# A graph-network kernel: column copies from octet 5 to the last octet, the second copy of x loaded an octet sooner, and the end in another order

## The chip, the cores and the metric

The kernel runs on one core of one Trainium2 chip. The metric is device time in microseconds (us), lower is better. A core has TensorE (PE, with its weight loads as PEld), VectorE (DVE), ScalarE (ACT), GpSimd (POOL) and SyncE (SP); POOL, SP and ACT also issue DMAs. Each engine works through its own instructions in order.

## What is computed

One layer of a graph network with a residual and a layer norm, over 12,500 nodes of 64 features and 400,000 edges with 16 features each; the edges come sorted by destination.

```python
def _L0_gnn_ref(x, edge_index, edge_attr, W1, b1, W2, b2, W3, b3):
    src, dst = (edge_index[0], edge_index[1])
    m_in = jnp.concatenate([x[src], x[dst], edge_attr], axis=-1)
    h = jax.nn.silu(m_in @ W1 + b1)
    messages = jax.nn.silu(h @ W2 + b2)
    agg = jax.ops.segment_sum(messages, dst, num_segments=x.shape[0])
    node_in = jnp.concatenate([x, agg], axis=-1)
    return jax.nn.silu(node_in @ W3 + b3)
...
x = _layernorm(x + _L0_gnn_ref(x, edge_index, edge_attr_16, ...), axis=-1)
```

## The kernel before

**Octets.** The edges are cut into 3,125 tiles of 128, and eight tiles make an octet: 391 octets (`NO`), numbered 0 to 390, the last with five tiles. One turn of the main loop `for o in range(NO + 2)` in `windows` stands for one octet. Two tiles make a pair, so an octet has four pairs, the last octet three. Many steps of one turn belong to neighbouring octets: gathers are issued three octets ahead (`AHEAD`), the second layer comes two later, the sums four, adding them into `agg` six. For the last eight octets (`DRAIN`) these lags are 1, 2 and 3, so some turns there do two second layers.

**Where the source rows come from.** `x[src] @ W1` for a tile can come in one of three ways. (1) A gather (`gather`, line 448): POOL issues one indirect DMA per tile that fetches 128 rows; up to octet 11 (`RAW` = 12) from `x` itself, from then on from `pa`, a table of products that the start writes to DRAM (`table`). (2) Column copies (`columns`, lines 367 and 369): the core holds two copies of `x` turned round, `xs` and `x2`, and ACT or DVE copies single columns of them, two edges at a time, into a tile `cx` that stands for a whole pair of tiles (256 edges, 128 copies). Before each 8 (ACT) or 16 (DVE) copies the engine loads the addresses into registers. (3) Single rows that SP copies (`rows`). A pair served by (2) or (3) needs two gathers fewer.

**What sets how many.** `shares` says how many edges' worth of columns an engine copies in an octet: ACT 80 in four octets of five and else 64, DVE 96 in seven of ten and else 64, none before octet `BEGIN`. From the running sums, `pairs` gives each engine a list of octets: when 256 more edges are done by octet `o`, a pair of octet `o + 2` is theirs, up to `len(octs) - QUIET - 2`. So `BEGIN` and `QUIET` set the first and the last octet with copies. The copies of an octet stand in fixed places between its other work: on ACT one block ahead of the first layer's silu (`h`, line 557) and one ahead of the second's (`m`, line 572); on DVE a block ahead of `xw` and `oh`, and two behind.

**An octet on its way.** `compare_nodes` (`eh`) and `turn`/`turned` (`ph`, `oh`) make one-hot matrices of the destinations. `first_layer` turns the gathered rows into PSUM (L550), multiplies the copied columns (L553) and adds the one-hots' product (L554); ACT makes `h`. `second_layer` (L566, L568) and ACT make `m`; `add_up` (L581, `pg`) sums over destinations; `add_window` (L592) adds that into `agg`.

**Nodes.** Groups of 512 nodes are finished behind the edges: `node_begin`, `node_x`, `node_sums` on PE, `node_silu` on ACT, `node_add`, `node_stats`, then `root` (a square root on ACT with its own function table), `inverse`, `divide` and `store`. The last two groups are `rest` (512 nodes) and `rest + 1` (212 nodes). In the kernel before, `node_sums(rest)` to `node_stats(rest)` and `limits` (bounds on the indices, which tell whether the general path has to run) stand in turn 390 ahead of its first layer; `verdict` and all of `rest + 1` come last, and root, inverse, divide and store of both groups together.

**Order.** PE, ACT, DVE and SP run in the order in which the loop is written (`manual_schedule`); POOL's gathers follow their own list. A gather waits for a free buffer `ga` (five of them) and for the landing of the gather eight before it.

**Start.** ACT issues the loads of `xs` (turns 0 and 1) and `x2` (`resident2`, turns 2 to 4) in pieces of 2,048 columns, 0.5 MB each; DVE clears the other halves of both tiles in turns 1 to 5 (line 812); turns 1 to 7 make the table `pa`.

## Time and profile before

| | |
|---|---|
| time of three runs | 3284.28 us median (3284.22 to 3288.53) |
| profiled execution | 3281.77 us, span from first to last instruction 3280.0 us |
| mean granted TensorE clock | 0.712 |
| busy: ACT, POOL, PE, DVE | 3106.6, 2462.5, 2460.8, 2063.0 us |
| gathers on POOL | 94 from `x`, 2501 from `pa` |
| column copies | ACT 14464, DVE 16256 |
| HBM read | 135.31 MB |

How to read it: a busy share is a mean over the whole span. Issue of DMAs, register loads and waits are not counted as busy, so an engine can be taken up without being busy. The rows of a timeline give start, duration, engine, line, operation and, in brackets, how long the engine had been idle before and what ended that.

### The profile page before, as it was taken

Reading aid. Unit: us, or ns where it says so; the run is one execution under the profiler, and the core shown is the slowest. Engines: PE = TensorE matmul, PEld = TensorE weight load, DVE = VectorE, ACT = ScalarE, POOL = GpSimd, SP = SyncE. Lnnn points to the kernel's source line nnn. Section 1 sums busy time; section 2 is a strip of 40 time slices with the busy share of each in tenths; the row PEclk is TensorE's granted clock in tenths of the full one; section 3 lists DMA queues with packets and bytes.
Section 4 is the critical chain, followed back from the end, with each engine's and each line's share of the span. In section 5 each row is a group of like instructions: output and inputs, shape, how many; then the busy total and the mean of one; then the engine's idle time right before and its main releaser. Section 6 shows DMA issues by size and latency. Waiting matters only on the chain. (4 is left out here: it accounts for less than half of the span.)

```text
span 3280.0 us, 88619 instructions
## 1 busy us (share of the span) xinstructions
PE 2460.8 (75%) x15346; PEld 1722.2 (53%) x15346; DVE 2063.0 (63%) x18554; ACT 3106.6 (95%) x15306; POOL 2462.5 (75%) x2603
## 2 busy tenths in 40 slices
PE   7776777777778778777777776777778877877786
PEld 5554555545555555555555554545555555555454
DVE  5566666666666666666666666666666666666662
ACT  2899999999999999999999999999999999999992
POOL 7777777777777777777777777777777777777775
PEclk7777667777666776676776777767677676667767
DMA  6211111111111111111111111111111111111111
GB/s 148 53 39 40 46 39 40 46 39 40 45 45 44 42 43 41 41 43 39 48 43 42 42 42 41 42 42 46 45 40 43 40 42 43 40 47 46 39 41 37
DMA packets 160767, 147.72 MB, mean 45 GB/s; under 512 B 103706, under 2 KB 113678, under 8 KB 159422
## 3 DMA queue, kind: packets, MB, share of 16 engines
q0 software_dynamic: 83040, 85.20, 11.7%
q1 hardware_dynamic: 62648, 47.00, 5.3%
q10 hardware_dynamic: 14502, 9.75, 1.4%
q14 instruction: 450, 3.69, 0.3%
q8 instruction: 127, 2.08, 0.3%
HBM read 135.31 MB, written 6.40 MB: 43 GB/s over the span
## 5 line engine op out<-in xcount | busy, mean ns | idle before, releaser
L448 POOL DMA_INDIRECT ga<-pa,sc x2501 | 2372.4, 949 | 762.7 <-issue 649.9
L367 ACT ACTIVATE cx<-xs,x 128x1 f32 x14464 | 2786.9, 325 | 24.0 <-issue 17.7
L369 DVE TENSOR_TENSOR cx<-xs,x 128x4 uint8 x16256 | 1309.3, 154 | 1095.2 <-issue 1075.1
L581 PEld LDWEIGHTS pg<-eh,m 128*64 128x64 f32 x6250 | 281.9, 175 | 928.0 <-DVE agg L592 758.6
L581 PE MATMUL pg<-eh,m 128*64 128x48 f32 x6250 | 336.4, 262 | 467.1 <-DVE agg L592 465.1
L568 PE MATMUL p<-w2d,h 128*128 128x128 f32 x3126 | 641.1, 369 | 0.0
L568 PEld LDWEIGHTS p<-w2d,h 128*128 128x128 f32 x3126 | 543.5, 262 | 159.0 <-issue 159.0
L554 PE MATMUL p<-oh,xw 128*128 128x512 f32 (+1 forms) x758 | 575.2, 853 | 0.0
L550 PE MATMUL p<-ident,ga 128*128 128x128 f32 x1251 | 313.6, 370 | 118.6 <-DMA ga<-pa,sc 117.9
L515 PE MATMUL ph<-identb,eh 128*96 128x128 bf16 x1563 | 221.6, 285 | 158.0 <-DVE oh L525 154.2
L550 PEld LDWEIGHTS p<-ident,ga 128*128 128x128 f32 x1251 | 229.3, 197 | 144.0 <-issue 126.0
L557 ACT ACTIVATE h<-p 128x512 f32<-128x512 f32 x391 | 242.0, 619 | 51.9 <-PE p L554 32.7
L572 ACT ACTIVATE m<-p 128x512 f32<-128x512 f32 x391 | 242.3, 620 | 43.6 <-PE p L568 38.3
L515 PEld LDWEIGHTS <-eh 128*96 128x96 bf16 x1563 | 160.4, 166 | 211.5 <-DVE oh L525 198.4
L525 DVE COPY oh<-ph 96x512 f32<-96x512 f32 x391 | 263.1, 673 | 1.6 <-PE ph L515 1.6
L472 PE MATMUL mm<-w1bb,xr 65*96 65x128 f32 x782 | 230.0, 390 | 6.2 <-DMA xr<-in_xt 3.8
L497 DVE TENSOR_TENSOR eh<-wrow,dc 128x384 f32<-128x384 f32 x392 | 212.4, 542 | 9.3 <-PE pg L581 5.5
L566 PE MATMUL p<-b2r,one 3*128 3x512 bf16 x391 | 188.4, 482 | 31.3 <-ACT m L572 31.1
L554 PEld LDWEIGHTS p<-oh,xw 128*128 128x128 f32 x758 | 173.9, 282 | 0.0
L472 PEld LDWEIGHTS mm<-w1bb,xr 65*96 65x96 f32 x782 | 145.8, 239 | 7.7 <-DMA xr<-in_xt 4.0
L553 PE MATMUL p<-cx,w1d 128*128 128x128 f32 x478 | 122.9, 365 | 0.0
L477 DVE TENSOR_TENSOR xw<-mm,mask 96x128 f32<-96x128 f32 x391 | 108.0, 276 | 17.4 <-PE mm L472 17.4
(106 smaller groups left out, 971.5 us busy)
## 6 DMA issues: line engine op xcount, KB each, us to landing
rx<-pa SPq DMA_DIRECT2D x6400, 0.2 KB
ga<-pa,sc POOLq DMA_INDIRECT x2501
oh<-in_attr SPq DMA_DIRECT2D x130, 192.0 KB
xr<-in_xt SPq DMA_DIRECT2D x391, 24.0 KB
cxi<-in_src_pair SPq DMA_DIRECT2D x240, 1.0 KB
xs<-in_xt ACTq DMA_DIRECT2D x6, 512.0 KB
pa<-v ACTq DMA_DIRECT2D x12, 256.0 KB
x<-in_xt ACTq DMA_DIRECT2D x6, 512.0 KB
```

The source lines that it names most:

```text
L367: nc.scalar.activation(cols[key][:, k:k + 1], word(i, xb, XADDR), AF.Identity, bias=word(i + 4, x2b, X2ADDR))
L369: nc.vector.tensor_tensor(t[:, 4 * k:4 * k + 4], at(i, xb, XADDR), at(i + 4, x2b, X2ADDR), op=OP.max)
L448: nc.gpsimd.indirect_dma_start(out=ga[:, i, :], out_offset=None, in_=x if o < RAW else pa[:, :], in_offset=bass.IndirectOffsetOnAxis(ap=sc ...
L472: nc.tensor.matmul(pw[:E, :], winrow[o], w1bb.rearrange("k s m -> k (s m)"), start=True, stop=True)
L515: nc.tensor.matmul(ph[:E, i, :], eh[:, i, :, 1], identb, start=(i == 0), stop=(i == k - 1), skip_group_check=True)
L525: nc.vector.tensor_copy(oh[:E, :], ph[:E, :(n + 1) // 2].rearrange("p i e -> p (i e)"))
L550: nc.tensor.matmul(p1[:, i, :], g2.rearrange("p s d -> p (s d)"), ident, is_transpose=True, start=(i == c), stop=False, skip_group_check=True)
L554: nc.tensor.matmul(p1[:, :k], xw[o % 3], oh, start=False, stop=True, skip_group_check=True)
L557: nc.scalar.activation(h[:, :k], p1[:, :k], AF.Silu)
L568: nc.tensor.matmul(p2[:, 2 * i:2 * i + 2, :].rearrange("p s d -> p (s d)"), h[:, i, :], w2d, start=False, stop=(i == k - 1), skip_group_ch ...
L572: nc.scalar.activation(m[:, :n2], p2[:, :n2], AF.Silu)
L581: nc.tensor.matmul(pg[s * D:(s + 1) * D, :], m[:, i, :], eh[:, i // 2, :, s], start=(i < 2), stop=(i >= n - 2), skip_group_check=True)
```

## The change

Five things. `BEGIN` goes from 6 to 5 and `QUIET` from 3 to 0, so the copies start one octet sooner and go on to serve the last octet. The loads of `x2` come in turns 1 to 3 instead of 2 to 4, and the clearing of the halves in turns 1 to 4, four pieces a turn, instead of 1 to 5. The end of group `rest` (sums, silu, add, statistics) and `limits` move from turn 390 to turn 389, ahead of its first layer; its root is now worked out on DVE by `newton` (twelve small operations) instead of on ACT, and its divide follows at once. `verdict` and the store of `rest` come in turn 390 behind the first layer, so only group `rest + 1` is left for the end. And of a store, the rows beyond the last multiple of 16 (5 of the last group's 53) go by ACT's queue instead of SP's.

```diff
--- before.py
+++ after.py
@@ -30,7 +30,7 @@
 THIRD = 4
 LAST = 6
 RAW = 12
-BEGIN = 6
+BEGIN = 5
 TABLES = 7
 ACOLS = (48, 32)
 VCOLS = (32, 0, 32, 32)
@@ -43,7 +43,7 @@
 HALF = 6144
 OVER = 304
 TURN = 195
-QUIET = 3
+QUIET = 0
 DRAIN = 8
 LAG = CT * P // 32
 AHEADS = 256
@@ -650,6 +650,20 @@
         def root(q0, q1):
             nc.scalar.activation(rstd[:, q0 * G:q1 * G], mv[:, q0 * G:q1 * G, 1], AF.Sqrt, bias=eps)
 
+        hb = nv.tile([P, G], F32, name="hb")
+        sq = nv.tile([P, G], F32, name="sq")
+
+        def newton(q):
+            y = rstd[:, q * G:(q + 1) * G]
+            nc.vector.tensor_scalar(hb, mv[:, q * G:(q + 1) * G, 1], 1e-5, -0.5, op0=OP.add, op1=OP.mult)
+            bits = y.bitcast(I32)
+            nc.vector.tensor_scalar(bits, hb.bitcast(I32), 1, None, op0=OP.logical_shift_right)
+            nc.vector.tensor_scalar(bits, bits, -1.0, float(0x5f3759df + 0x3fc00000), op0=OP.mult, op1=OP.add)
+            for _ in range(3):
+                nc.vector.tensor_tensor(sq, y, hb, op=OP.mult)
+                nc.vector.tensor_tensor(sq, sq, y, op=OP.mult)
+                nc.vector.scalar_tensor_tensor(y, sq, 1.5, y, op0=OP.add, op1=OP.mult)
+
         def inverse(q0, q1):
             nc.vector.reciprocal(rstd[:, q0 * G:q1 * G], rstd[:, q0 * G:q1 * G])
 
@@ -662,9 +676,9 @@
         def store(q):
             c, n = groups[q]
             to, p = out[c:c + n, :].rearrange("(p i) d -> p i d", i=G), n // G
-            for a, b in ((0, p // 16 * 16), (p // 16 * 16, p)):
+            for a, b, eng in ((0, p // 16 * 16, nc.sync), (p // 16 * 16, p, nc.scalar)):
                 if b > a:
-                    nc.sync.dma_start(to[a:b], v[a:b, q % (2 * RB)])
+                    eng.dma_start(to[a:b], v[a:b, q % (2 * RB)])
 
 
 
@@ -769,8 +783,8 @@
                 if o < 2:
                     for c in parts[2:5] if o == 0 else parts[5:]:
                         resident(c)
-                if 2 <= o < 5:
-                    for c in parts[3 * o - 6:3 * o - 3]:
+                if 1 <= o < 4:
+                    for c in parts[3 * o - 3:3 * o]:
                         resident2(c)
                 if o == 3:
                     for s in range(2):
@@ -805,7 +819,7 @@
                     add_window(q)
                 if o == 1:
                     relative(0, CT, SCT)
-                for k in range(3 * o - 3, 3 * o) if 1 <= o < 6 else []:
+                for k in range(4 * o - 4, 4 * o) if 1 <= o < 5 else []:
                     if k < 2 * len(parts):
                         c = parts[k // 2]
                         t, w = (x2[:D], N) if k % 2 else (xs[D:], NP)
@@ -824,15 +838,22 @@
                     behind()
                     for q in folds[NO]:
                         add_window(q)
+                if o == NO - 2:
                     for i in range(G):
                         node_sums(rest, i)
                     node_silu(rest)
                     node_add(rest)
                     for i in range(G):
                         node_stats(rest, i)
+                    newton(rest)
+                    for i in range(G):
+                        divide(rest, i)
                     bad = limits()
                 if o < NO:
                     first_layer(o)
+                if o == NO - 1:
+                    verdict(bad)
+                    store(rest)
                 for f, a in todo.get(o, []) if o < NO else []:
                     if f is node_silu:
                         f(*a)
@@ -883,16 +904,15 @@
                 for q in folds.get(i, []):
                     add_window(q)
             assert NO not in todo
-            verdict(bad)
             for i in range(G):
                 node_sums(rest + 1, i)
             node_silu(rest + 1)
             node_add(rest + 1)
             for i in range(G):
                 node_stats(rest + 1, i)
-            root(rest, NG)
-            inverse(rest, NG)
-            for q in range(rest, NG):
+            root(rest + 1, NG)
+            inverse(rest + 1, NG)
+            for q in range(rest + 1, NG):
                 for i in range(G):
                     divide(q, i)
                 if q == NG - 1:
```

On POOL, the number of gathers falls by six:

```order
-L448 DMA ga<-in_x,sc 128x64 x94
-L448 DMA ga<-pa,sc 128x64 x2501
```

```order
+L448 DMA ga<-in_x,sc 128x64 x92
+L448 DMA ga<-pa,sc 128x64 x2497
```

ACT has one pair more (128 copies), DVE two (256). With the octets' numbers from `pairs`, a gather's count by octet from 381 to 390 is 8, 4, 8, 8, 4, 8, 8, 6, 8, 5 before and 4, 8, 8, 4, 8, 8, 4, 6, 8, 3 now.

On DVE, turns 386 and 387 (`cx` is the tile of copied columns, `cxi` the addresses, `oh` the next octet's one-hots), the difference of the two orders:

```order
 L592 TENSOR_TENSOR agg<-agg,pg 128x48 x2
 L497 TENSOR_TENSOR eh<-wrow,dc 128x384
-L477 TENSOR_TENSOR xw_169<-mm,mask 96x128
-L525 COPY oh<-ph 96x512
+L350 TENSOR_LOAD cxi
+L369 TENSOR_TENSOR cx<-xs,x_100 128x4 x16
+L477 TENSOR_TENSOR xw_169<-mm,mask 96x128
+L525 COPY oh<-ph 96x512
+L350 TENSOR_LOAD cxi
+L369 TENSOR_TENSOR cx<-xs,x_100 128x4 x16
+L350 TENSOR_LOAD cxi
+L369 TENSOR_TENSOR cx<-xs,x_100 128x4 x16
```

Where these turns had no copies, there are now 16 ahead of the next octet's `xw` and `oh` and 32 behind them; turns 383 and 384 get the same, turn 385 gets 16 and 16, and 16 remain in turn 387.

On DVE, around the last octet's one-hots (`oh` with 384 columns), before:

```order
L525 COPY oh<-ph 96x512
L660 TENSOR_SCALAR v<-v,mv,rstd 128x64 x4
L592 TENSOR_TENSOR agg<-agg,pg 128x48
L525 COPY oh<-ph 96x384
L660 TENSOR_SCALAR v<-v,mv,rstd 128x64 x4
```

and now, the last twelve rows of what stands there:

```order
L674 TENSOR_SCALAR v<-v,mv,rstd 128x64 x4
L721 TENSOR_SCALAR xs<-rowi 128x144 x3
L724 TENSOR_TENSOR xs<-xs,wb 128x391
L726 TENSOR_REDUCE lim<-lims 128x1
L727 TENSOR_REDUCE lim<-lims 128x1
L728 TENSOR_REDUCE lim<-xs 128x1
L729 TENSOR_REDUCE lim<-xs 128x1
L731 TENSOR_SCALAR bad<-lim 128x1
L732 TENSOR_SCALAR bad<-lim 128x1
L733 TENSOR_SCALAR bad<-lim 128x1
L734 TENSOR_SCALAR bad<-lim 128x1
L525 COPY oh<-ph 96x384
```

Between L592 and `oh` there are now group `rest`'s add, four pairs of statistics, `newton`, four divides (the first row here) and `limits`.

On PE, the last two octets (`p` of L550 to L554 is a first layer, of L566 and L568 a second, L630 to `wrow` is `node_sums(rest)`), before:

```order
L566 MATMUL p_197628<-b2r,one_120 128x512
L568 MATMUL p_197628<-w2d,h 128x128 x4
L630 MATMUL wrow<-w3s,agg 128x64 x4
L550 MATMUL p_197670<-ident,ga 128x128 x3
L554 MATMUL p_197670<-oh,xw_169 128x384
```

and now:

```order
L566 MATMUL p_199637<-b2r,one_120 128x512
L568 MATMUL p_199637<-w2d,h 128x128 x4
L550 MATMUL p_199646<-ident,ga 128x128 x2
L553 MATMUL p_199646<-cx,w1d 128x128
L554 MATMUL p_199646<-oh,xw_169 128x384
```

The four products of `node_sums(rest)` have left the way between octet 389's second layer and octet 390's first; they stand ahead of octet 389's first layer. One of octet 390's gathered pairs has become a pair of copied columns.

## The prediction

> **What bounds the kernel now.** I read the page first, then the gathers' line, the waits of POOL and ACT, the stretches around the end, and the timeline from 3180 us on.
>
> ```profile
> PE 2460.8 (75%) x15346; PEld 1722.2 (53%) x15346; DVE 2063.0 (63%) x18554; ACT 3106.6 (95%) x15306; POOL 2462.5 (75%) x2603
> ...
> L448 POOL DMA_INDIRECT ga<-pa,sc x2501: 940/944/1377, 122.0 to 3255.9; - x193
> ...
> POOL ga L448 <- issue: 676.1, 2217, 0.3
> POOL ga L448 <- PE p L545: 2.0, 2, 1.7
> ...
> ACT m L572 <- PE p L568: 6.5, 11, 1.4
> ```
>
> ACT looks like the bound with 95%, but POOL with its 75% is the engine that never rests. Its 2501 gathers start from 122.0 to 3255.9 us, one every (3255.9 - 122.0) / 2500 = 1.2536 us: 0.944 us of work and 0.30 us of "issue" behind each. In the waits hardly one is longer than those 0.3 us; the longest is 1.7 us. So the last gather's time is about the number of gathers times 1.25 us, whatever the other engines do, as long as buffers come free. The last row is ACT's longest wait for PE in total from 600 to 3100 us: 6.5 us in 2500. ACT too is full there, and hardly behind POOL; the two are balanced.
>
> What happens at the end:
>
> ```profile
> 3180.00:3200.00 20.00, 15.34 (x91) 10.65 (x91) 12.00 (x99) 18.97 (x93) 15.12 (x17) 0.65 0.15 33
> 3200.00:3220.00 20.00, 15.78 (x82) 11.06 (x81) 2.96 (x11) 3.17 (x6) 15.12 (x17) 0.52 0.17 40
> 3220.00:3240.00 20.00, 15.49 (x141) 10.30 (x139) 6.06 (x21) 6.37 (x9) 15.12 (x17) 0.80 0.21 56
> ...
> 3239.64 0.94 POOL L448 DMA_INDIRECT ga<-pa,sc  x1 [0.30 <-issue]
> 3248.55 0.37 PE L515 MATMUL ph<-identb,eh 128*96 128x128 bf16 x3
> 3249.66 0.94 POOL L448 DMA_INDIRECT ga<-pa,sc  x1 [0.30 <-issue]
> 3252.20 0.45 PE L550 MATMUL p<-ident,ga 128*128 128x128 f32 x1 [2.19 <-DMA ga<-pa,sc]
> 3254.44 0.60 ACT L557 ACTIVATE h<-p 128x512 f32<-128x512 f32 x1 [6.28 <-PE p L554]
> 3258.45 1.16 PE L568 MATMUL p<-w2d,h 128*128 128x128 f32 x8
> 3259.44 1.98 PE L630 MATMUL wrow<-w3s,agg 128*128 128x64 f32 x8
> 3261.02 0.49 PEld L550 LDWEIGHTS p<-ident,ga 128*128 128x128 f32 x3
> 3262.43 0.49 ACT L557 ACTIVATE h<-p 128x384 f32<-128x384 f32 x1 [0.60 <-PE p L554]
> 3263.67 0.49 DVE L707 TENSOR_SCALAR xs<-rowi 128x144 f32<-128x144 int32 x3
> 3264.22 0.49 ACT L572 ACTIVATE m<-p 128x384 f32<-128x384 f32 x1 [1.30 <-PE p L568]
> 3266.13 0.19 DVE L592 TENSOR_TENSOR agg<-agg,pg 128x48 f32 x1
> 3266.47 0.84 PE L581 MATMUL pg<-eh,m 128*64 128x48 f32 x10 [2.34 <-DVE agg L592]
> 3267.61 1.11 PE L630 MATMUL mm<-w3s,agg 128*53 128x64 f32 x8 [0.17 <-DVE agg L592]
> ```
>
> The columns of the stretches are PE, PEld, DVE, ACT, POOL, the granted clock, the DMA share and GB/s. At 3200 us the copies end: ACT falls from 18.97 to 3.17 us in 20, DVE from 12.00 to 2.96, and POOL stays at 15.12. From there POOL alone sets the time: octet 389's last gather starts at 3249.66, PE waits 2.19 us for it, and `h` follows at 3254.44. Behind that comes a chain of single steps to the end, of which the change shortens three.
>
> **The change part by part.** The sum is made against the profiled execution (span 3280.0, time 3281.77); it is 2.51 us below the median of the runs, 3284.28, and I take the same difference off both.
>
> *Gathers, -5.0 us.* Up to octet 389 there are now four fewer (2586 instead of 2590), so its last one starts 4 x 1.2536 = 5.0 us sooner, at 3244.65. The two that octet 390 saves, 2.5 us more, gain nothing: the last now starts at 3255.9 - 7.5 and lands at 3250.9, and PE gets to it at 3254.6 (below).
>
> *The copies that replace them, 0.* At the start ACT's 40 new copies and DVE's 48 fall into idle time:
>
> ```profile
> 79.86 0.60 ACT L557 ACTIVATE h<-p 128x512 f32<-128x512 f32 x1 [4.63 <-PE p L545]
> 98.21 0.60 ACT L572 ACTIVATE m<-p 128x512 f32<-128x512 f32 x1 [2.98 <-PE p L568]
> 77.96 0.69 DVE L544 COPY m<-mm 128x512 f32<-128x512 f32 x1 [5.29 <-PE mm L542]
> 84.19 0.20 DVE L592 TENSOR_TENSOR agg<-agg,pg 128x48 f32 x1 [4.75 <-PE pg L581]
> 87.95 4.56 ACT L367 ACTIVATE cx<-xs,x 128x1 f32 x24 [0.85 <-issue]
> ...
> 3162.39 1.31 DVE L369 TENSOR_TENSOR cx<-xs,x 128x4 uint8 x16 [0.69 <-issue]
> 3165.12 1.29 DVE L369 TENSOR_TENSOR cx<-xs,x 128x4 uint8 x16 [1.42 <-issue]
> ```
>
> 24 of ACT's copies last 4.56 us and stand where it waited 4.63, 16 last two thirds of that, 3.0, where it waited 2.98. DVE needs 3165.12 - 3162.39 = 2.73 us for 16 with their register load, and waited 5.29 and 4.75. At the end ACT's other 88 copies go to the two octets in which it had come to rest. DVE gets 208 more, 13 blocks or 35 us, in turns 382 to 387. From 3200 to 3240 us it was idle 40 - 2.96 - 6.06 = 31 us. So DVE comes out of these turns about 35 - 31 = 4 us later than now, near 3232 in turn 387. Octet 388's last gather, at 3239.64 - 5.0 = 3234.6, lands 2.5 us later (as 3249.66 to 3252.20 shows for octet 389), at 3237, and is what its first layer waits for. Bounds: nothing, or 4 us when that slack is not there. I take nothing.
>
> A rule of the Trainium skill speaks against more copies: in "SBUF — State Buffer", section "Who interferes with whom", a VectorE instruction with two inputs in SBUF keeps out a GpSimd instruction that reads SBUF. By that rule the new copies would lengthen gathers. The stretches above bear on it: 17 gathers take 15.12 us beside 12.00 us of DVE work as well as beside 2.96. It is a rival below.
>
> *The end in another order, -2.7 us.* On PE, octet 390's first layer no longer stands behind `node_sums(rest)`: it can start when the second layer before it ends, 3258.45 + 1.16 = 3259.61, instead of 3261.02, -1.4 us; a pair of copied columns costs some 0.3 us more than the gathered pair it replaces (an estimate between nothing and 0.5: two products of 128 columns in place of one turned pair). That makes -1.1. What was in the way goes ahead of octet 389's first layer, where PE waits for gathers anyway, so its 1.98 us are covered.
>
> ```profile
> 3256.88 0.60 ACT L572 ACTIVATE m<-p 128x512 f32<-128x512 f32 x1 [1.83 <-PE p L568]
> 3257.53 0.67 PE L581 MATMUL pg<-eh,m 128*64 128x48 f32 x16 [0.75 <-ACT m L572]
> 3261.45 0.38 ACT L636 ACTIVATE z<-wrow 128x256 f32<-128x256 f32 x1 [1.15 <-PE wrow L630]
> 3261.87 0.42 DVE L642 TENSOR_TENSOR v<-xa,z 128x256 f32<-128x256 f32 x1 [3.42 <-ACT z L636]
> 3265.88 0.15 DVE L717 TENSOR_SCALAR bad<-lim 128x1 f32<-128x1 f32 x1
> 3271.61 1.87 DVE L660 TENSOR_SCALAR v<-v,mv,rstd 128x64 f32<-128x64 f32 x8
> L667 SPq DMA_DIRECT2D out<-v x26: 331/375/874, 894.3 to 3274.0; - x26
> ```
>
> On DVE the same group and `limits` now stand ahead of the last `oh`. Their length from the rows of the end: add and statistics 3261.87 to 3263.67, 1.8 us; four divides 1.0; `limits` 3263.67 to 3266.13, 2.5; `newton` has no row: twelve operations of 128 x 4 at 0.06 (four tiny ones take from 3265.88 to 3266.13) to 0.23 us (a divide, 1.87 / 8), 0.7 to 2.8, and I take 2.0, since they depend on each other. Together 7.3 us. The sums can start once octet 390's `ph` is done: at 3248.92 now, and some 4.2 us sooner then, a little less than the gathers, for the copies' sake: 3244.7. With 1.98 for the sums and 0.38 for the silu, DVE starts at 3247.1 and `oh`, after 0.6 of its own, ends near 3255.0. PE wants it 0.5 us after 3259.6 - 5.0, at 3255.1. Hidden, with no slack: late by up to 2 us if `newton` is at its upper bound or the sums start later.
>
> `limits` out of the last stretch: `pg` of octet 390 waits 2.34 us for the add L592, which stood behind `limits` on DVE until 3266.13. From `m` to `pg` are 2.25 us now; one octet before it was 3257.53 - 3256.88 = 0.65. That gives -1.6.
>
> *The last divides and stores, -1.6 us.* Four divides instead of eight: half of 1.87, -0.9. SP's last issue starts at 3274.0 and takes up to 0.87 us; it now stands on ACT beside SP's: -0.7 (between -0.4 and -0.9). The root of `rest + 1` with its table load stays; `verdict` and the store of `rest`, in turn 390 now, have nothing behind them on PE and SP but this same end, and are covered by its layers.
>
> *The loads of x2 an octet sooner, +0.8 us.*
>
> ```profile
> 40.00:60.00 20.00, 18.43 (x107) 13.79 (x106) 14.26 (x15) 4.48 (x8) 14.02 (x16) 0.84 1.00 214
> 23.74 1.76 DVE L812 MEMSET x<- 64x2048 f32 x1 [0.46 <-issue]
> 51.65 0.94 POOL L448 DMA_INDIRECT ga<-in_x,sc  x1 [0.30 <-DMA ga<-in_x,sc]
> 54.31 0.94 POOL L448 DMA_INDIRECT ga<-in_x,sc  x1 [1.72 <-PE p L545]
> ```
>
> While the loads of `x2` run, the DMA engines are full (share 1.00) and POOL has its one real stall, 1.4 us beyond the usual pitch. Three of them, 1.5 MB, now follow two of `xs` at once: at 214 GB/s about 10 us of queue. A gather waits for the one eight before it, which allows 10 us less its usual landing of some 2.5. So a stall of up to 3 us is new, and the old one may go: between -1.4 and +3, I take +0.8. The clearing puts a fourth memset (1.76 and 0.46 us) into DVE's turns 1 to 3 and takes it out of 4 and 5; first layers there come some 2 us later, which POOL, several octets ahead, does not feel.
>
> Sum: -5.0 - 1.1 - 1.6 - 1.6 + 0.8 = -8.5. The span would be 3271.5, the profiled execution 3273.3, the median **3275.8 us**.
>
> **The rivals.**
>
> *The copies at the end set the pace.* For it: DVE's 35 us of blocks meet 31 us of idle time, and ACT is as full as POOL until then. Against: the gathers' own pace of 8 an octet (10 us) leaves DVE room. If the slack is not there, octets 388 and 389 come 4 us later: 3279.8.
>
> *The block ahead of the last `oh` shows.* `newton` at 2.8 us and the sums 1.7 us later: 2.5 us late, 3278.3.
>
> *Slower: the gathers starve behind the loads at the start.* The place is turns 1 and 2, the price that of one queue of the last five loads of `xs` and six of `x2`: 5.2 MB at 214 GB/s are 24 us; less the 7.5 that a gather may be late, POOL would stand 16.5 us instead of 1.4. That adds 15 to the gathers' end: 3275.8 - 0.8 + 15 = 3290. It beats the gain when POOL stalls over 9.3 us more than now. Against it: under a full DMA load POOL lost 1.4 us. The Trainium skill, "DMA: Bandwidth & Descriptors", section "Queues, rings and completion order", has each DMA engine take turns between queues packet by packet, by which gathers would not starve.
>
> *Copies keep POOL out*, by the rule named above. If each of DVE's 256 new copies held a gather for its own 1.29 / 16 = 0.08 us, that is 20.6 us: 3296. The stretches above show nothing of it.
>
> *The change does not do what it says*, that POOL is not what ends the octets: then only the end's 4.3 us come: 3280.
>
> **How the numbers follow.** A difference under 0.2% (6.6 us) can't be told from none here. Chances: forecast 0.72; copies at the end 0.10; block before `oh` 0.05; POOL not the bound 0.06; gathers starving 0.06; copies keeping POOL out 0.01. Below 3277.7 lies 0.69 of the forecast's 0.72 (its own range is 3272 to 3279), and none of the others: faster 0.69, same 0.24, slower 0.07. The range runs from 3271.5 (stall gone, all terms at their better bound) to 3281.0, which takes in the rivals but the two slower ones.
>
> **What would show it.** Right: 2589 gathers with the same 1.25 us pitch, the last one near 3249 us; the last `pg` within 0.7 us of its `m`; four divides at the end. Octet 389's `h` near 3249.4 confirms the gathers' term, octet 390's near 3256.3 the order. Wrong: POOL gaps over 3 us before 60 us; `p` L554 of octets 386 to 388 waiting for `oh` or `cx` of DVE instead of for gathers; octet 390's L554 waiting for `oh`.

## The result and the profile after

The changed kernel took 3293.36 us, median of ten runs (3289.03 to 3297.89), beside 3284.25 for the kernel before: a ratio of 1.0025, 95% interval 1.0017 to 1.0033. Two later measurements gave 1.0002 (0.9993 to 1.0011) and 1.0030 (1.0019 to 1.0040). The forecast was 3275.8 with a range up to 3281.0. The profiled execution took 3289.7 us, span 3287.9, 7.9 more than before.

The page's busy line, and the line of the gathers:

```profile
PE 2472.1 (75%) x15349; PEld 1746.5 (53%) x15349; DVE 2081.1 (63%) x18825; ACT 3149.9 (96%) x15434; POOL 2460.5 (75%) x2597
...
L448 POOL DMA_INDIRECT ga<-pa,sc x2497: 940/944/1377, 119.9 to 3252.7; - x193
```

The gathers did what was foretold in kind: 2589 of them, and the last starts 3.2 us sooner (3255.9 before). The stretches before the end, in the same columns as before:

```profile
3180.00:3200.00 20.00, 16.39 (x101) 10.87 (x100) 12.93 (x123) 20.00 (x101) 15.15 (x16) 0.62 0.18 42
3200.00:3220.00 20.00, 12.87 (x83) 8.77 (x82) 12.00 (x111) 20.00 (x101) 15.24 (x16) 0.72 0.18 41
3220.00:3240.00 20.00, 14.93 (x129) 10.66 (x128) 12.64 (x118) 11.75 (x39) 15.12 (x16) 0.77 0.20 50
```

ACT no longer drops to 3 us in 20 at 3200, and VectorE not to 2.96. Then the timeline of the last octets:

```profile
54.97 0.94 POOL L448 DMA_INDIRECT ga<-in_x,sc  x1 [2.33 <-DMA ga<-in_x,sc]
...
3242.80 0.38 DVE L592 TENSOR_TENSOR agg<-agg,pg 128x48 f32 x2
3248.97 0.94 POOL L448 DMA_INDIRECT ga<-pa,sc  x1 [0.30 <-issue]
3256.59 2.03 PE L630 MATMUL wrow<-w3s,agg 128*128 128x64 f32 x8
3259.08 0.43 DVE L642 TENSOR_TENSOR v<-xa,z 128x256 f32<-128x256 f32 x1 [3.85 <-ACT z L636]
3260.02 0.60 ACT L557 ACTIVATE h<-p 128x512 f32<-128x512 f32 x1 [0.98 <-PE p L554]
3261.00 0.17 DVE L658 TENSOR_SCALAR hb<-mv 128x4 f32<-128x4 f32 x1
3262.03 0.60 ACT L572 ACTIVATE m<-p 128x512 f32<-128x512 f32 x1 [1.41 <-PE p L568]
3263.38 0.98 DVE L674 TENSOR_SCALAR v<-v,mv,rstd 128x64 f32<-128x64 f32 x4
3266.76 0.54 DVE L525 COPY oh<-ph 96x384 f32<-96x384 f32 x1
3268.11 0.19 DVE L592 TENSOR_TENSOR agg<-agg,pg 128x48 f32 x1
3268.45 1.09 PE L581 MATMUL pg<-eh,m 128*64 128x48 f32 x16 [6.52 <-DVE agg L592]
3272.18 0.60 ACT L572 ACTIVATE m<-p 128x512 f32<-128x512 f32 x1 [9.55 <-PE p L568]
3273.99 0.49 ACT L557 ACTIVATE h<-p 128x384 f32<-128x384 f32 x1 [1.21 <-PE p L554]
3275.90 0.49 ACT L572 ACTIVATE m<-p 128x384 f32<-128x384 f32 x1 [1.42 <-PE p L568]
3276.44 0.55 PE L581 MATMUL pg<-eh,m 128*64 128x48 f32 x10 [0.64 <-ACT m L572]
```

Two things stand in it. Octet 389's last gather starts at 3248.97, its `h` comes at 3260.02: 11 us behind, where before it was 4.8 (3249.66 to 3254.44). Octet 389 doesn't wait for its gathers any more. And VectorE's block runs from 3259.08 to the end of `oh` at 3267.3; behind it stands `add_window(387)` (3268.11), and for that PE's `pg` of octet 388 waits 6.52 us, although its `m` was made at 3262.03. Octet 389's second layer stands behind that `pg`, so its `m` comes 9.55 us late and octet 390's `h` 14.0 us behind octet 389's, where it was 8.0. Behind that `h` the end is shorter: 13.9 us instead of 17.6.

### The profile page after: what moved, and what is told of

Read it like the earlier page. It is cut to its first block, busy times and chain, and to the rows that moved or that the text cites. A ratio compares the mean times of both kernels' runs of the same rounds, so it can differ in the third digit from the quotient of the medians.

```text
span 3287.9 us, 89055 instructions
## 1 busy us (share of the span) xinstructions
PE 2472.1 (75%) x15349; PEld 1746.5 (53%) x15349; DVE 2081.1 (63%) x18825; ACT 3149.9 (96%) x15434; POOL 2460.5 (75%) x2597
## 3 DMA queue, kind: packets, MB, share of 16 engines
q8 instruction: 127, 2.08, 0.3%
## 5 line engine op out<-in xcount | busy, mean ns | idle before, releaser
L367 ACT ACTIVATE cx<-xs,x 128x1 f32 x14592 | 2859.3, 358 | 16.2 <-issue 11.9
L369 DVE TENSOR_TENSOR cx<-xs,x 128x4 uint8 x16512 | 1328.1, 156 | 1123.4 <-issue 1101.1
L581 PE MATMUL pg<-eh,m 128*64 128x48 f32 x6250 | 329.7, 259 | 555.7 <-DVE agg L592 554.4
L568 PE MATMUL p<-w2d,h 128*128 128x128 f32 x3126 | 646.5, 371 | 0.0
L568 PEld LDWEIGHTS p<-w2d,h 128*128 128x128 f32 x3126 | 547.5, 264 | 180.4 <-issue 180.4
L554 PE MATMUL p<-oh,xw 128*128 128x512 f32 (+1 forms) x758 | 581.9, 863 | 0.0
L550 PE MATMUL p<-ident,ga 128*128 128x128 f32 x1249 | 300.7, 376 | 1.7 <-DMA ga<-pa,sc 1.7
L572 ACT ACTIVATE m<-p 128x512 f32<-128x512 f32 x391 | 254.5, 651 | 37.7 <-PE p L568 37.5
L557 ACT ACTIVATE h<-p 128x512 f32<-128x512 f32 x391 | 254.1, 650 | 29.7 <-PE p L545 17.0
L550 PEld LDWEIGHTS p<-ident,ga 128*128 128x128 f32 x1249 | 236.2, 204 | 1.9 <-issue 1.9
L566 PE MATMUL p<-b2r,one 3*128 3x512 bf16 x391 | 186.5, 477 | 52.9 <-ACT m L572 52.6
L554 PEld LDWEIGHTS p<-oh,xw 128*128 128x128 f32 x758 | 175.4, 284 | 0.0
```

Of the source, the lines that this page charges most:

```text
L367: nc.scalar.activation(cols[key][:, k:k + 1], word(i, xb, XADDR), AF.Identity, bias=word(i + 4, x2b, X2ADDR))
L369: nc.vector.tensor_tensor(t[:, 4 * k:4 * k + 4], at(i, xb, XADDR), at(i + 4, x2b, X2ADDR), op=OP.max)
L550: nc.tensor.matmul(p1[:, i, :], g2.rearrange("p s d -> p (s d)"), ident, is_transpose=True, start=(i == c), stop=False, skip_group_check=True)
L554: nc.tensor.matmul(p1[:, :k], xw[o % 3], oh, start=False, stop=True, skip_group_check=True)
L557: nc.scalar.activation(h[:, :k], p1[:, :k], AF.Silu)
L568: nc.tensor.matmul(p2[:, 2 * i:2 * i + 2, :].rearrange("p s d -> p (s d)"), h[:, i, :], w2d, start=False, stop=(i == k - 1), skip_group_ch ...
```

## The experiments

The profiles of one kernel differ by some us at the start (below), so beside the ratios I use four measures from each profile. In the table: when octet 29's `h` comes; how long from there to octet 380's; how far octet 389's `h` lies behind the start of its last gather; and how long from that `h` to the end of the span. All ratios here lie within 1% of 1. In the expectations, group 23 is `rest`, and the letters of the theories are given anew in each.

| kernel | octet 29 | 29 to 380 | 389 behind gather | 389 to end | ratio to before (95%) |
|---|---|---|---|---|---|
| before | 285.5 | 2892.1 | 4.8 | 25.6 | |
| before_c | 288.7 | 2890.5 | 3.9 | 24.8 | |
| loads_only | 291.6 | 2891.2 | 6.1 | 25.5 | 0.9997 (0.9988 to 1.0006) |
| begin_only | 293.7 | 2893.5 | 4.8 | 28.1 | 0.9992 (0.9983 to 1.0001) |
| quiet_only | 290.6 | 2890.9 | 4.4 | 26.0 | 0.9993 (0.9984 to 1.0002) |
| copies_b | 293.8 | 2895.2 | 19.1 | 26.0 | 0.9997 (0.9988 to 1.0006) |
| end_only | 301.0 | 2890.7 | 7.6 | 26.7 | 1.0001 (0.9992 to 1.0010) |
| changed | 291.0 | 2895.4 | 11.0 | 27.9 | 1.0025 (1.0017 to 1.0033) |
| after_b | 300.4 | 2895.0 | 17.4 | 27.9 | 1.0002 (0.9993 to 1.0011) |
| after_c | 288.3 | 2894.2 | 12.5 | 28.1 | 1.0030 (1.0019 to 1.0040) |
| after_less | 291.1 | 2895.5 | 14.0 | 27.7 | 1.0036 (1.0023 to 1.0050) |
| moved_b | 299.9 | 2893.9 | 12.5 | 24.1 | 0.9999 (0.9990 to 1.0008) |
| split_b | 293.3 | 2892.3 | 10.5 | 22.9 | 0.9983 (0.9974 to 0.9992) |
| split_less | 289.9 | 2892.7 | 10.2 | 21.7 | 0.9989 (0.9980 to 0.9998) |

after_b and after_c are the changed kernel again, before_c the kernel before. Ratios of one measurement (the parts; after_b, copies_b, moved_b, split_b; after_c, after_less, split_less) share a chip and can be compared with each other; across measurements a comparison is weaker.

### The parts, one at a time

Of the change's diff, `end_only` keeps everything but the constants and the two lines of the loads:

```diff
 # against the changed kernel
-BEGIN = 5
+BEGIN = 6
-QUIET = 0
+QUIET = 3
-if 1 <= o < 4:
-    for c in parts[3 * o - 3:3 * o]:
+if 2 <= o < 5:
+    for c in parts[3 * o - 6:3 * o - 3]:
-for k in range(4 * o - 4, 4 * o) if 1 <= o < 5 else []:
+for k in range(3 * o - 3, 3 * o) if 1 <= o < 6 else []:
```

> The kernel before with nothing but the new order of the end (group 23, newton, divide and limits in turn 389 ahead of the first layer, verdict and store in turn 390, four divides, the last store on ACT's queue); copies and loads as before. Theory A, the block stands in front of the wrong thing: on VectorE its 7.7 us (3259.08 to 3266.76 in the profile of the changed kernel) also lie ahead of add_window(387), for which pg of octet 388 waits, and behind that stands octet 389's second layer. Then h of octet 390 comes 3 to 5 us later than 3262.43, pg L581 waits over 5 us for agg L592 shortly before it, and the stretch from that h to the end is 3.7 us shorter (13.9 instead of 17.6): 3284.5, between 3282 and 3287. Theory P, the prediction's terms for the end hold and something else was lost: -4.3, 3280. Theory C, the new order is the whole loss: over 3290.

It came out as 1.0001, so theory C fell and so did P (3280 is 0.9987). The profile has what A expects, although the copies end early here:

```profile
3256.81 0.95 POOL L448 DMA_INDIRECT ga<-pa,sc  x1 [0.30 <-issue]
3264.38 0.60 ACT L557 ACTIVATE h<-p 128x512 f32<-128x512 f32 x1 [2.17 <-PE p L554]
3269.93 0.54 DVE L525 COPY oh<-ph 96x384 f32<-96x384 f32 x1
3271.62 1.09 PE L581 MATMUL pg<-eh,m 128*64 128x48 f32 x16 [5.34 <-DVE agg L592]
3277.22 0.49 ACT L557 ACTIVATE h<-p 128x384 f32<-128x384 f32 x1 [1.26 <-PE p L554]
```

`pg` of octet 388 waits 5.34 us for the add behind the block, octet 390 comes 12.8 us behind octet 389, and from there to the end are 13.9 us.

`quiet_only` is the kernel before with one line:

```diff
-QUIET = 3
+QUIET = 0
```

> The kernel before with QUIET 0 alone: one more pair of octet 388 for ACT and one for VectorE, four gathers fewer (2591), all of them ahead of octet 389; start and end as before. Theory A, from the moment the copies no longer stop early, ACT's and VectorE's own chains set the octets and the gathers don't: ACT's copies go on to about 3227, the octets behind them follow at 6 us each, octet 389's h at 3251 to 3255 instead of 3254.44 although its last gather starts 5.0 us sooner: 3281 to 3285. Theory P, gathers set the time: -5.0, 3279.3. Theory D, the copies at the end are the whole loss: over 3288.

0.9993: some 2 us, not told from nothing; theory D fell, A's range fits, and P's 3279.3 (0.9985) lies at the interval's edge. In the profile A's octet 389 (3251 to 3255) fell: its last gather starts at 3243.91, its `h` comes at 3248.31, so the gathers' term is at work there. That profile is of the fastest of eleven executions, 3276.19 us beside a median of 3286.82, so it doesn't stand for all of them.

```profile
3243.91 0.95 POOL L448 DMA_INDIRECT ga<-pa,sc  x1 [0.30 <-issue]
3248.31 0.60 ACT L557 ACTIVATE h<-p 128x512 f32<-128x512 f32 x1 [2.16 <-PE p L554]
```

`loads_only` and `begin_only` are the kernel before with the change's two lines of the loads, the second with `BEGIN = 5` as well.

> The kernel before with the second copy of x loaded an octet sooner and cleared at four memsets a turn in turns 1 to 4, nothing else. Theory A, the start is what the octets hang on: octets 2 to 5 come 4 to 6 us later (their table products fall into a stretch with full DMA engines and a granted clock of 0.50), ACT never makes that up since it is full from octet 6 on, and of it 2 to 6 us are left at the end: 3286 to 3290. Theory P: POOL is several octets ahead and only its own stall counts: +0.8, 3285.1, between 3283 and 3288. Theory D, the loads gain by taking the old stall away: 3283.

> The kernel before with BEGIN 5 and the earlier loads and memsets that it needs, QUIET 3 and the old end: 2591 gathers, one more pair for ACT and VectorE, used by octet 387. Theory A: as loads_only by octet 5, and then some 2 us more since octet 5's copies are not all hidden; at the end the gathers of octet 389 are 5.0 us sooner, and the octets come when ACT's and VectorE's chains let them, h of octet 389 at 3252 to 3257: 3283 to 3288. Theory P: -5.0 + 0.8, 3280. Theory D, copies from octet 5 are the whole loss: over 3290.

0.9997 and 0.9992. Theory D fell for the copies from octet 5; A's better end and P are both within the interval there. For the loads A fell but for its lowest end, and neither P's +0.8 nor D's gain is told from nothing. Nor is the late start shown to be the loads' doing. In the kernel before, the second turn's 32 table products took 3.78 us, and in the changed kernel 7.09, but so they do in end_only, whose start is that of the kernel before:

```profile
45.78 7.09 PE L209 MATMUL mm<-w1ab,xs 64*128 64x64 f32 x32
```

```profile
40.00:50.00 10.00, 9.22 (x30) 6.17 (x29) 5.57 (x7) 1.56 (x3) 7.56 (x9) 0.50 0.94 198
```

The clock granted there was 0.50; in the two profiles of the kernel before it was 0.83 and 0.67 in the same stretch, so the start differs between executions of one kernel. With old loads octet 29 comes at 285.5 to 301.0, with new ones at 288.3 to 300.4; a difference of some us between the two kinds wouldn't be seen in this. (The 28.1 us of begin_only's end go with a low clock too: PE was granted 0.50 to 0.63 from 3250 us on, and eight products of L568 took 2.08 us, where the kernel before needs 1.16.)

### Together, and with the order undone or mended

`copies_only` is the changed kernel without the new end. `after_moved` moves VectorE's block one place:

```diff
 for q in folds.get(o, []) if o != NO else []:
     add_window(q)
+if o == NO - 1:
+    node_add(rest)
+    ...                  # statistics, newton, divides, limits
 ...
 if o == NO - 2:
     for i in range(G):
         node_sums(rest, i)
     node_silu(rest)
-    node_add(rest)
-    ...
```

`split_end` has `BEGIN` 6, `QUIET` 0 and the loads of before, and this end:

```diff
+if o == NO - 1:                       # behind add_window(387)
+    bad = limits()
+if o == NO + 1:                       # behind add_window(389)
+    newton(rest, 0, 8)
 ...
 node_silu(rest + 1)
+newton(rest, 8, 12)
+for i in range(G):
+    divide(rest, i)
+store(rest)
```

with `node_sums` to `node_stats` of `rest` back where the kernel before has them, and `verdict` where the changed one has it. They were first run, beside the changed kernel, on a chip on which the kernel before took 4959.5 us:

> The changed kernel itself, beside its parts: its own slowdown of 1.0025 was measured in another session than the four parts, none of which cost anything (ratios 1.0001, 0.9993, 0.9997, 0.9992). Theory A, the parts interact: the new order of the end needs VectorE at rest in turns 387 to 389, and the copies that no longer stop early take that rest away: again 1.0015 to 1.0035. Theory S, the parts simply add up: 0.9985 to 0.9999, and the 1.0025 was the session's.

> The changed kernel without the new order of the end (BEGIN 5, QUIET 0 and the earlier loads stay, 2589 gathers). Theory A, copies and order cost only together: not slower than before, ratio 0.998 to 1.0005, the last gather early and the octets behind it held by VectorE's copies to about 3246, octet 390's h some 8 us behind octet 389's instead of 13.96. Theory K, the copies at the end alone are the loss (VectorE is behind from turn 385 on, whatever the order): 1.002 to 1.0035, like the changed kernel.

> The changed kernel with VectorE's block (node_add, statistics, newton, divides, limits) one place later, behind the copy of the last oh, the batch's last divides and add_window(387), and ahead of add_window(388); the sums and the silu of group 23 stay ahead of octet 389's first layer. Theory A, pg of octet 388 waited 6.52 us for add_window(387) behind the block and with it octet 389's second layer and octet 390: pg of 388 now follows its m at once, h of octet 390 comes about 7 us behind octet 389's instead of 13.96, and what is still late is pg of 389 behind add_window(388): 5 to 7 us faster than the changed kernel, ratio to before about 1.000 to 1.001. Theory K, VectorE's copies before it are the loss: no more than 1 to 2 us faster than the changed kernel.

> BEGIN 6, QUIET 0, loads as before (the kernel quiet_only, ratio 0.9993), and an end put together from the traces: group 23's sums, silu, add and statistics where the kernel before has them, limits on VectorE right behind add_window(387) where it waits 2.6 us for pg of 388, eight of newton's twelve operations behind add_window(389), the other four and the four divides of group 23 behind add_window(390) while the last sums and silu run, verdict behind octet 390's first layer, the last store on ACT's queue. Theory A, each piece fills a wait: limits out of the last stretch -1.6, four divides -0.7, the last store -0.7, together -3.0 against quiet_only: ratio to before about 0.9984 (0.9975 to 0.9993). Theory N, what stands behind these waits isn't on the path: as quiet_only, 0.9993. Theory D, newton's pieces push add_window(390) out: slower than quiet_only by 1 to 3 us.

The ratios there were 1.0050 (1.0037 to 1.0064), 1.0057 (1.0044 to 1.0070), 1.0035 (1.0022 to 1.0048) and 1.0006 (0.9997 to 1.0015). Against the expectations, the changed kernel and the copies alone were slower than A has them (the copies alone as K has them), and split_end missed its 0.9984. That chip runs the kernel in another regime (last section), so nothing is carried over from it; moving the block took 7.4 us off the median there, with intervals that overlap. The same four kernels on an ordinary chip:

> The changed kernel beside its parts, on a chip of ordinary speed. Theory A, the parts interact (the new order needs VectorE at rest in turns 387 to 389, and the copies that no longer stop early take that rest away): 1.0015 to 1.0035. Theory S, the parts add up: 0.9985 to 0.9999.

> BEGIN 5, QUIET 0 and the earlier loads, without the new order of the end. Theory A: not slower than before, 0.998 to 1.0005, and octet 390's h some 8 us behind octet 389's instead of 13.96. Theory K, the copies at the end alone are the loss: 1.002 to 1.0035. On the slow chip, where ACT and VectorE were the bound throughout, it was as slow as the changed kernel (1.0057 and 1.0050), which is what K expects of a kernel bound by them.

> The changed kernel with VectorE's block behind the last oh and add_window(387) and ahead of add_window(388). Theory A: pg of 388 follows its m at once, h of octet 390 about 7 us behind octet 389's instead of 13.96; 5 to 7 us faster than the changed kernel, ratio to before 1.000 to 1.001 (on the slow chip it was 7 us faster, 4980.7 against 4988.0). Theory K: at most 2 us faster than the changed kernel.

> BEGIN 6, QUIET 0, loads as before, and the end put together from the waits (limits behind add_window(387), newton in two pieces behind add_window(389) and add_window(390), divides of group 23 there, last store on ACT's queue). Theory A: -3.0 against quiet_only, ratio to before about 0.9984, between 0.9975 and 0.9993. Theory N, these pieces weren't on the path: 0.9993, as quiet_only. Theory D, newton's pieces push add_window(390) out: 1.000.

The changed kernel came out as 1.0002, copies_b as 0.9997, moved_b as 0.9999: three kernels whose times can't be told apart. So A missed for the changed kernel (1.0015 to 1.0035), K missed for copies_b (1.002 to 1.0035), and moved_b was 2.1 us faster than the changed kernel, where A has 5 to 7 and K at most 2. Their profiles can be told apart. In copies_b the octets lie 19.1 us behind the gathers, with VectorE still copying at 3248, and the old end takes its usual 26.0 us:

```profile
3241.85 0.94 POOL L448 DMA_INDIRECT ga<-pa,sc  x1 [0.30 <-issue]
3248.08 1.26 DVE L369 TENSOR_TENSOR cx<-xs,x 128x4 uint8 x16 [1.53 <-issue]
3260.98 0.60 ACT L557 ACTIVATE h<-p 128x512 f32<-128x512 f32 x1 [2.16 <-PE p L554]
3268.66 0.49 ACT L557 ACTIVATE h<-p 128x384 f32<-128x384 f32 x1 [0.71 <-PE p L554]
```

In moved_b `pg` of octet 388 follows its `m` at once and octet 390's `h` 5.9 us behind octet 389's:

```profile
3267.99 0.60 ACT L557 ACTIVATE h<-p 128x512 f32<-128x512 f32 x1 [0.98 <-PE p L554]
3270.64 0.67 PE L581 MATMUL pg<-eh,m 128*64 128x48 f32 x16 [0.75 <-ACT m L572]
3273.85 0.49 ACT L557 ACTIVATE h<-p 128x384 f32<-128x384 f32 x1 [0.43 <-PE p L554]
3276.69 0.67 PE L581 MATMUL pg<-eh,m 128*64 128x48 f32 x16
```

Now `pg` of octet 389 is late instead, at 3276.69: `add_window(388)` stands behind the block on VectorE (3276.35), and on PE `verdict`, which comes first, waits 2.68 us for the result of `limits`. The end takes 24.1 us, 3.8 less than the changed kernel's 27.9. That the block stood in front of `pg` of octet 388 is shown; that it cost 3.8 us rests on the profiles, since the 2.1 us between the medians aren't clear of noise.

split_b is faster than both kernels, 0.9983, as its theory A had it (0.9984). `pg` of octets 388 and 390 starts 0.65 and 0.54 us behind the start of `m`, the divides of `rest` run on VectorE beside the last sums and the last silu, and the end takes 22.9 us:

```profile
3266.30 0.67 PE L581 MATMUL pg<-eh,m 128*64 128x48 f32 x16 [0.75 <-ACT m L572]
3273.66 0.55 PE L581 MATMUL pg<-eh,m 128*64 128x48 f32 x10 [0.64 <-ACT m L572]
3274.51 1.01 PE L630 MATMUL mm<-w3s,agg 128*53 128x64 f32 x8 [0.30 <-DVE agg L592]
3275.15 0.98 DVE L678 TENSOR_SCALAR v<-v,mv,rstd 128x64 f32<-128x64 f32 x4
3278.46 0.98 DVE L678 TENSOR_SCALAR v<-v,mv,rstd 53x64 f32<-53x64 f32 x4
```

### Which engine carries the octets

```diff
-return ACOLS if (o - BEGIN) % 5 < 4 else (ACOLS[0] - 16, ACOLS[1])
+return ACOLS if (o - BEGIN) % 5 < 4 and not 200 <= o < 220 else (ACOLS[0] - 16, ACOLS[1])
```

takes one pair, 128 copies, from ACT in the middle; split_less is split_end with the same line.

> The changed kernel as the measure for the next one: ratio to before 1.000 to 1.003, octet 389's h 10 to 18 us behind its last gather.

> The changed kernel with one pair of columns fewer on ACT, out of octets 200 to 219 (16 of them have 32 copies instead of 40): 14464 copies on ACT instead of 14592, 2591 gathers instead of 2589, the end as it is. Theory A, ACT's copies carry the octets from octet 7 on: its chain gets 128 x 0.19 = 24 us shorter, until the gathers, 2.5 us later and with a margin of 11 to 18 us over the 4.8 that they need, catch it: 4 to 10 us faster than the changed kernel. Theory P, the gathers carry it: 2.5 us slower. Theory D, VectorE is as full as ACT: within 2 us.

> split_end (BEGIN 6, QUIET 0, pieces of the end in the waits; ratio 0.9983 on an ordinary chip) with the same pair taken from ACT: 2593 gathers, 14464 copies on ACT, 16384 on VectorE. Theory A: its margin over the gathers was 10.5 us against 4.8, of which 2.5 go to the two gathers, so 0 to 4 us faster than split_end, ratio 0.997 to 0.9983. Theory P: 2.5 us slower, 0.999. Theory D: 0.9983.

> The kernel before once more, for a second profile. Theory A: the start is drawn anew with the clock that PE is granted; octet 29's h comes at 286 to 301 us instead of 285.5, the octets from there to 380 take 2891 to 2893 us whatever the gathers do, and octet 389's h lies 4.8 to 8 us behind its last gather. Theory P: the start doesn't matter, the last gather near 3249.7 plus or minus what the gathers' own pitch gives, h 4.8 us behind it.

Theory A fell here: with 128 copies (24 us by the expectation) less for ACT, after_less was 1.0036 beside 1.0030 for the changed kernel, with 2895.5 us from octet 29 to 380 as before. The times don't tell P (2.5 us slower) from D (within 2 us); the 14.0 us between octet 389's last gather and its `h` speak against P. The windows around the removed copies show more, first the changed kernel (after_c), then after_less:

```profile
1700.00:1800.00 100.00, 71.61 (x443) 50.63 (x443) 64.29 (x583) 98.10 (x489) 75.89 (x80) 0.69 0.20 41
```

```profile
1700.00:1800.00 100.00, 71.52 (x448) 50.35 (x446) 63.79 (x584) 85.64 (x410) 75.61 (x81) 0.71 0.19 41
```

ACT's work falls from 98.10 to 85.64 us of 100, and VectorE still gets through 584 instructions instead of 583. The waits of VectorE in that stretch of after_less:

```profile
DVE cx L369 <- issue: 36.1, 32, 1.9
```

63.79 us busy and 36.1 us in front of copies, where it waits for nothing that the trace shows and loads its registers: 99.9 of 100. VectorE is taken up whole there, at a busy share of 64%.

The same holds for the kernel before, and PE's waits show who waits for whom. From 600 to 3100 us, the kernel before:

```profile
DVE cx L369 <- issue: 867.1, 818, 1.9
...
PE pg L581 <- DVE agg L592: 389.7, 194, 4.8
PE ph L515 <- DVE oh L525: 135.2, 150, 2.2
PE p L550 <- DMA ga<-pa,sc: 86.4, 61, 2.9
```

and the changed kernel:

```profile
PE pg L581 <- DVE agg L592: 458.4, 214, 4.5
...
PE ph L515 <- DVE oh L525: 132.3, 151, 2.3
```

In the kernel before VectorE was busy for 1609.0 of these 2500 us and stood 867.1 in front of copies, 2476.1 together. PE waited 525 us for VectorE and 86.4 for gathers, and 74.4 of the 86.4 lie behind 2600 us. In the changed kernel it waited for no gather in this stretch. So VectorE set PE's pace in both kernels, and the gathers took over only late in the kernel before, and not at all in the changed one.

split_less, 0.9989 beside 1.0030 for the changed kernel, has a ratio within the interval of split_b's 0.9983, which is from another chip: no gain from ACT's pair is shown there either, and P's 0.999 fits as well as D. before_c is a second profile of the kernel before, with octet 29 at 288.7 and the gathers deciding the end, 3.9 us ahead of the `h`, as theory A and P both had it within an us.

The counterpart, one pair fewer on VectorE (32 instead of 48 copies in eight of octets 200 to 210) or on both:

```diff
-return VCOLS if n == 3 else VCOLS[:3] + (0,)
+return VCOLS if n == 3 and not 200 <= o < 211 else VCOLS[:3] + (0,)
```

> The changed kernel with one pair of columns fewer on VectorE, out of octets 200 to 210 (eight of them have 32 copies instead of 48): 16384 copies instead of 16512, 2591 gathers, the rest as it is. The measure is the time from octet 29's h to octet 380's, which was 2893.5 to 2895.5 us in every profile with BEGIN 5, and the margin of octet 389's h over its last gather, 11 to 18 us. Theory D, VectorE carries the octets: its chain gets 8 blocks of 2.73 us = 22 us shorter; 2875 to 2885 us, until ACT or the gathers catch it, the kernel 5 to 10 us faster than the changed kernel (ratio to before 0.998 to 1.0005). Theory E, ACT and VectorE are equally full: within 3 us of 2895 and the time within 2 us. Theory P, gathers: 2.5 us slower.

> The changed kernel with one pair fewer on each of ACT and VectorE in the same octets: 14464 and 16384 copies, 2593 gathers. Theory E: now both chains are 22 to 24 us shorter and the octets run until the gathers, 5 us later, catch them: octet 29 to 380 in 2885 to 2890 us, octet 389's h 5 to 8 us behind its last gather, 3 to 8 us faster than the changed kernel. Theory D: as after_lessv, less 2.5 us for the gathers. Theory N, neither carries them: 2895 again, 5 us later at most.

Both fell to a chip of the slow kind (the kernel before took 4867.1 us there): 1.0068 (1.0055 to 1.0082) and 1.0065 (1.0052 to 1.0079). They say nothing on an ordinary chip. That VectorE carries the octets is thus read from its full time and from PE's waits, and that ACT alone doesn't is shown by after_less; that a lighter VectorE would make the kernel faster was not shown.

## Why the prediction was wrong

**What bounds the kernel now** is the step that failed first. It was right that the gathers end the kernel before (4.8 and 3.9 us from last gather to `h` in two profiles), wrong that they do so with room to spare: that POOL never rests tells when a gather starts, not that an octet waits for it. VectorE's 63% was passed over; with its register loads it was taken up for 2476.1 of 2500 us, and ACT was busy for 2473.0 of them. In the kernel before an octet's `h` lay 17.1 us behind its last gather at octet 29, 11.6 at octet 200, 5.4 at octet 380 and 4.8 at octet 389: the gathers, with 2903.8 us from octet 29 to 380 where the octets took 2892.1, caught up only near the end. In the changed kernel it was 21.6, 18.9, 10.1 and 11.0, so gathers that start sooner had nothing to give. From octet 29 to 380 every profile on an ordinary chip needs 2890.5 to 2895.5 us, whether octet 389 comes 4 or 19 us behind its gathers.

**Gathers, -5.0.** In the profile of the changed kernel octet 389's last gather came at 3248.97 instead of the foretold 3244.65, and its `h` at 3260.02 instead of 3249.4. Against before: 5.5 us later by octet 29, 3.3 more by octet 380, 3.2 less from there to octet 389. The first is within the spread of the start and isn't shown to be the change. Of the second some belongs to the change: all seven profiles with `BEGIN` = 5 need 2893.5 us or more from octet 29 to 380, all seven with 6 need 2892.7 or less; which engine's copies make it isn't shown. The last is what was left of the -5.0. In quiet_only's profile the `h` does follow its last gather at 4.4 us.

**The copies that replace them, 0.** VectorE's turn 387 began at 3242.80, not near 3232. Of that, 8.8 us were carried along from octet 380 and some 7 were lost in its last turns, where 4 was reckoned. The rival that names this (copies at the end set the pace) had the place right and, at +4, half the size.

**The end in another order, -2.7** is the second step that failed: "Hidden, with no slack" looked only at `oh`. The trace shows the block in front of `add_window(387)` as well, then `pg` of octet 388, octet 389's second layer and octet 390. And the 1.98 us of the sums were not covered: they took 2.03 us ahead of octet 389's first layer, where PE no longer waited for gathers. From octet 389's `h` to the end the sum had 21.3 us (25.6 less 4.3); it took 27.7 to 28.1 in four profiles and 26.7 in end_only, against 24.8 to 26.0 in five of the six profiles with the old end. So of the 16.4 us by which the profiled span (3287.9) missed the sum's 3271.5, 6.6 lie behind octet 389's `h`, 5.5 ahead of octet 29's, 3.3 from there to octet 380's, and 1.0 between octets 380 and 389, where the sum had -4.2 with the loads. Where the block is out of the way of octet 388's `pg` (moved_b), octet 390's `h` comes 5.9 us behind octet 389's, against 8.0 in the kernel before: there PE's -1.1 came, and more. `newton` was sized well: twelve operations from 3261.00 to 3263.38, 2.4 us for 2.0.

**Limits, divides, stores, -3.2** came, and a little more: from octet 390's `h` to the end 3.7 us less, `pg` 0.54 us behind the start of `m` instead of 2.25, four divides.

**The loads of x2, +0.8**: the stall is 2.33 us where it was 1.72. Starving gathers did not happen. The trace agrees with the Trainium skill, "DMA: Bandwidth & Descriptors", section "Queues, rings and completion order", by which each DMA engine takes turns between queues. Nor did copies keep POOL out: 16 or 17 gathers fill 15.12 to 15.24 us of 20 beside 12 us of VectorE.

**What stays open** is the size. The changed kernel took 3290 to 3293 us in all three measurements on ordinary chips, the kernel before 3281.5, 3284.3 and 3288.5. Where gathers took 947 ns instead of 944, 2500 of them are 7.5 us longer, which a kernel that waits for them feels and the changed one doesn't. That could explain the three ratios; the profiles don't cover the runs that it would need. The parts ran on one chip, where before took 3289.2, and copies_b on the one with 3288.5, so that the parts alone cost nothing on the faster chips isn't shown.

## What to carry to other kernels

Count an engine as taken up by its busy time plus the time in which it issues or loads registers, before calling it idle: three engines at 63, 75 and 95% were all nearly full here, and taking work from ACT, the one with 95%, gained nothing. Look also at how far each step lies behind the one that is said to hold it: an engine that never rests needn't be the one that the others wait for. When a block moves ahead of a step, list everything that stands behind it on that engine and who waits for each, not just the step that it was moved past. A block of 8 us can be cut to the lengths of the waits that the trace shows: with the copies to the end that gave split_b and split_less, the only two whose intervals lie below the kernel before; on the slow chip the same kernel was no faster (1.0006).

## What the runs showed of the hardware

On two of the chips the same kernel took 4959.5 and 4867.1 us. Instructions there were no longer than elsewhere (a copy on ACT 281 ns beside 358 in the changed kernel's first profile, a gather 945), but ACT and VectorE stood still between them, at the same moments:

```profile
2000.67 0.29 ACT L367 ACTIVATE cx<-xs,x 128x1 f32 x1 [0.38 <-issue]
2000.68 0.16 DVE L369 TENSOR_TENSOR cx<-xs,x 128x4 uint8 x1 [1.18 <-issue]
2001.39 0.29 ACT L367 ACTIVATE cx<-xs,x 128x1 f32 x1 [0.43 <-issue]
2001.40 0.16 DVE L369 TENSOR_TENSOR cx<-xs,x 128x4 uint8 x1 [0.56 <-issue]
```

```profile
L367 ACT ACTIVATE cx<-xs,x 128x1 f32 x14592 | 2856.4, 281 | 536.9 <-issue 502.3 <-DVE eh L497 7.9 <-DMA rx<-pa 5.9
L448 POOL DMA_INDIRECT ga<-pa,sc x2497 | 2359.4, 945 | 2417.7 <-PE p L550 1401.4 <-issue 654.1 <-remote 220.1
```

Single copies 0.72 us apart, where elsewhere 16 follow each other in 3.1 us, and gathers that wait 1401.4 us for PE. What the two engines waited for isn't in the trace. And the gathers' median differs between profiles, 944 to 947 ns, as in the kernels with the same 2501 gathers, before (944) and end_only, whose last ones start 7.2 us apart:

```profile
L448 POOL DMA_INDIRECT ga<-pa,sc x2501: 941/947/1312, 122.4 to 3263.1; - x193
```
